# One ring of four PSUM banks, squares of keys from SBUF, and a new order of steps in a cross-attention and quantized feed-forward layer

## The chip, the cores and the metric

The kernel runs on one core of one Trainium2 chip. The metric is the device time of one execution in microseconds, given as the median of several runs. The engines of the core are TensorE (PE: matrix products and transposes, which write only to PSUM; PEld is its loading of weights), VectorE (DVE), ScalarE (ACT), GpSimd (POOL) and SyncE (SP), whose queue issues every transfer of this kernel. PSUM has eight banks; a bank holds one tile of 512 float32 columns on 128 partitions.

## The reference

The layer works on 8 batches of 112 tokens of width 512, with 375 context rows of width 256 for each batch. Attention has 16 heads of 128.

```python
def _L0_xattn_ref(hidden_states, encoder_hidden_states, Wq, Wk, Wv, Wo, gq, gk):
    def rmsnorm(x, g, eps=EPS):
        var = jnp.mean(jnp.square(x), axis=-1, keepdims=True)
        return x * jax.lax.rsqrt(var + eps) * g
    ...
    q = (hidden_states @ Wq).reshape(B, Sq, H, D)
    k = (encoder_hidden_states @ Wk).reshape(B, Skv, H, D)
    v = (encoder_hidden_states @ Wv).reshape(B, Skv, H, D)
    q = rmsnorm(q, gq)
    k = rmsnorm(k, gk)
    scores = jnp.einsum('bqhd,bkhd->bhqk', q, k) * scale
    attn = jax.nn.softmax(scores, axis=-1)
    out = jnp.einsum('bhqk,bkhd->bqhd', attn, v)
    return out.reshape(B, Sq, H * D) @ Wo
...
x = x + _L0_xattn_ref(_layernorm(x, axis=-1), ctx_1024, ...)
x = x + _L0_ffn_ref(_layernorm(x, axis=-1), ...)
```

The feed-forward part rounds its input to 8-bit integers by rows and its weights by one scale, multiplies by W1 (512 to 2048), adds a bias, applies GELU, rounds again by rows, multiplies by W2 (2048 to 512) and adds a bias.

## The kernel before

**Units.** The work is cut into 16 groups G (four pairs of batches times four groups of four heads) and 32 units u (a group and one batch of its pair). A group of four heads is 512 columns wide, which is one bank. A step is a small piece of work on one unit, group or batch, named by letters and a number: `k1.7` makes the second of three tiles of keys of unit 7. Numbers behind the dot are relative to the pair of batches that a script plays; `w0.-1` belongs to the last unit of the pair before.

**The steps of a unit and their engines.** On PE, `k0`, `k1`, `k2` make three tiles of keys (`pkk`, L655). ACT copies each to SBUF (`kc`, into `kk`, L675) and squares it (`kq`, into `ksq`, L681); both read the bank. DVE sums the squares (`kr`, L687); `ka`, `kb`, `ke`, `kd` take the inverse root (ACT and DVE); `kn` scales the keys in `kk` (L694), `kt` transposes their 32 by 32 blocks into `kz` (L704), `ks` sends these to DRAM and `kf` fetches them back as the full transpose `kT`. `kk` has two buffers, so the copies of unit u+2 need the block transposes of unit u to be done. Then come the scores `s0` to `s3` (L764, four banks of their own), their maxima `x` on DVE, exponentials `e` and scaling `n` on ACT, block transposes `z`, and transfers `ps` and `pf`, which give `pT`. `w0`, `w1` weigh the context rows with it (`pu`, L866), and `v0`, `v1` copy the result out (L877). For a group, `Q0`, `Q1` make the queries (`pq`, L537); `S` squares them (L552), `qt` transposes blocks, `qs` and `qf` transfer, `G` applies the gains. `o`, `u` make and copy the values (`po`, L893, L903), `p`, `a` project and add (`pw`, L916, L932); at the very end `O`, `U`, `P`, `A` do the same by halves. `kv`, `qw`, `pt`, `xt`, `ct` and `tp` are transposes on PE, used in the first units, for the last probabilities and in the last feed-forward steps.

**The feed-forward part** of a batch takes the sum of the projections (`ra` or a transfer), adds it to x (`rb`), takes statistics (`st`), an inverse root (`fa` to `fd`), normalizes (`fi`), rounds (`fq`), transposes (`ti`, `tj`, or a transfer), makes the hidden tiles (`h0` to `h3`, L1086; `i`, L1095), applies GELU (`g`), finds the largest (`mx`, `es`), rounds (`qp` on DVE, `qq` on ACT), transposes (`tp`, `tk`), and multiplies by W2 (`Y`, or `y0` and `y1`, L1165; `yo` adds, L1172; `yd` sends).

**What sets the order.** Four scripts, one for each pair, list all steps by hand-written words. `play` (L201) runs them in that order, and `in_written_order` (L77) ties each instruction of PE, DVE, ACT and SP to the one before it on its engine. Nothing overtakes on an engine: an instruction that waits holds up all behind it. Waits between engines follow from tiles: a new tile in a pool waits until the readers of the tile that had its buffer are done.

**PSUM.** Of the eight banks, four hold scores (`ps_sc`), three form a ring `ps_mm` for all products and some transposes, and one, `ps_tr`, holds the warm-up product, transposes at the start (`xt`, `ct`), and some at the end (`ra` of the even batch, `ti`, even `tp`).

Of the kernel before, what the change touches and what calls it, by code (L numbers as in the profile page):

```python
# [30 lines left out]
def xattn_ffn_kernel(  # L31
# [61 lines left out]
    ps_mm = ctx.enter_context(tc.tile_pool(name="ps_mm", bufs=3, space=PSUM))  # L93
    ps_tr = ctx.enter_context(tc.tile_pool(name="ps_tr", bufs=1, space=PSUM))
# [5 lines left out]
    def tr_tile(name):  # L100
        return ps_tr.tile([P, NW], F32, tag="tr", name=name)

    def trh_tile(name, i):
        pool, tag = ((ps_tr, "tr"), (ps_mm, "mm"))[i % 2]
        return pool.tile([P, 2 * NW], BF16, tag=tag, name=name)
# [13 lines left out]
    pw = tr_tile("warm")  # L119
# [279 lines left out]
    def token_turn(b):  # L399
        after(("xm", b))  # L400
        pt = T["pxn", b] = tr_tile(f"pxn_{b}")
        for k in range(KC):
            nc.tensor.transpose(
                pt[:, k * S : (k + 1) * S], tokens_of(b)[:, k * P : (k + 1) * P], ident[:S, :S]
            )
# [67 lines left out]
    def rows_turn(b, j0, j1):  # L473
        pt = T["pc", b] = tr_tile(f"pc_{b}_{j0}")
        for j in range(j0, j1):
            for k in range(KCC):
                nc.tensor.transpose(
                    pt[:, (j - j0) * CC + k * P : (j - j0) * CC + (k + 1) * P],
                    T["cT", b][:, k, j * P : (j + 1) * P], ident,
                )  # L480
# [196 lines left out]
    def key_squares(u, j):  # L677
        if u == 0:
            after(("kh", 1))
        sq = T["ksq", u, j] = work.tile([P, GW], F32, tag="ksq", name=f"ksq_{u}_{j}")  # L680
        nc.scalar.activation(sq, T["pkk", u, j][:, :GW], AF.Square)  # L681
# [280 lines left out]
    def turn_sum(b):  # L962
# [6 lines left out]
        pa = T["pa", b] = (tr_tile, mm_tile)[i](f"pa_{b}")  # L969
# [84 lines left out]
    def turn_rows(what, b, k0, n, i):  # L1054

        pt = T["pt", what, b, k0] = trh_tile(f"p{what}_{b}_{k0}", i)
# [13 lines left out]
    def turn_in(b):  # L1070
        turn_rows("xq", b, 0, KC, 0)
# [73 lines left out]
    def turn_piece(b, n):  # L1145
        after((f"qq{n}", b))
        turn_rows("hq", b, n * (NW // P), NW // P, n)
# [65 lines left out]
    for n in range(2):  # L1213
# [7 lines left out]
        cz.0 lk.0 cz.1 lf.0 lf.1 lx.0 l7.0 lc.1 gl.0 kh.0 lv.0 lk.1 jl.0 lq.0 kh.1 xs.0 xs.1 xa.0 cz.2  # L1221
        xs.7 ct0.0 xa.1 lc.2 xc.1 kc0.0 lq.1 xb.1 xb.7 kq0.0 jl.3 xb.0 kq2.0 k0.1 kr0.0 kc1.0 kr2.0
        kq1.0 xd.1 xc.0 ck0.0 k1.1 xd.0 xa.7 xm.1 kq0.1 xm.0 xc.7 kc2.0 kr1.0 xt.0 xd.7 k2.1 ka.0 ke.0
        kb.0 xk.0 kd.0 kc0.1 kn1.0 kq1.1 xt.1 xm.7 kc1.1 kr0.1 kv1.0 xk.1 kn0.0 kq2.1 xt.7 gm.0 kc2.1
        kn2.0 kv0.0 xk.7 kr1.1 xy.0 k0.2 xl.0 kw0.0 lk.2 kw1.0 lx.1 jm.0 kv2.0 Q0.0 kw2.0 kr2.1 kb.1
        ka.1 ke.1 xy.1 kd.1 kq0.2 kn2.1 kc0.2 kn1.1 k1.2 kn0.1 kt0.1 ct0.1 kc1.2 kt1.1 kq1.2 Q1.0 kt2.1
        ck0.1 qt0.0 ks.1 kr0.2 jm.3 qv0.0 qs0.0 S0.0 jl.1 jl.2 cb0.2 qw0.0 S1.0 k2.2 qv1.0 sb.0 kr1.2
        qx0.0 s3.0 kq2.2 s2.0 sa.0 sc.0 kc2.2 sd.0 ct1.0 s0.0 ck1.0 s1.0 qt1.0 xs.3 qw1.0 qs1.0 kf.1
        kr2.2 k0.3 jl.6 kb.2 ly.0 ka.2 x0.0 ke.2 Q0.1 x1.0 e0.0 kq0.3 kd.2 qx1.0 kr0.3 e2.0 kn2.2 e3.0
        e1.0 k1.3 S0.1 iv.0 kn0.2 kc0.3 kn1.2 n1.0 k2.3 qt0.1 n0.0 cb1.2 qs0.1 n2.0 kt0.2 kq1.3 s2.1  # L1230
        kt2.2 kq2.3 kc1.3 ct1.1 kr2.3 pt0.0 kc2.3 kt1.2 pt1.0 pk0.0 s3.1 n3.0 ks.2 pk1.0 s0.1 kr1.3 s1.1
        x1.1 ka.3 pt3.0 pt2.0 x0.1 lq.2 Q1.1 s7.0 lk.3 pk3.0 e0.1 jm.1 pk2.0 e2.1 e1.1 k0.4 ke.3 e3.1
        kb.3 kd.3 S1.1 kn0.3 kf.2 w0.0 iv.1 qf0.1 kn2.3 n3.1 kq0.4 qt1.1 n0.1 kt0.3 qs1.1 n1.1 kr0.4
        k1.4 xa.3 n2.1 z0.1 sa.1 z2.1 kc0.4 z1.1 kq1.4 k2.4 z3.1 v0.0 sb.1 kc1.4 ps.1 kt2.3 k0.5 kn1.3
        kc2.4 sc.1 kt1.3 kr1.4 ks.3 w1.0 sd.1 jm.2 G0.1 kq2.4 s0.2 lo.0 s1.2 kr2.4 Q0.2 kb.4 ka.4 xs.2
        xc.3 ke.4 v1.0 ja.0 kd.4 kc0.5 pf.1 kn0.4 kq0.5 qf1.1 ck1.1 x0.2 s3.2 e0.2 s2.2 e1.2 kt0.4 kf.3
        k1.5 S0.2 kn2.4 kr0.5 Q1.2 qt0.2 kq1.5 x1.2 qs0.2 js.0 e2.2 kc1.5 e3.2 k2.5 lq.3 kt2.4 S1.2 s7.1
        xb.3 xd.3 iv.2 kn1.4 w0.1 n1.2 lk.4 n0.2 kt1.4 G1.1 z0.2 ks.4 n3.2 js.2 n2.2 jr.0 s3.3 s0.3 cs.2
        qt1.2 s2.3 kq2.5 kr1.5 sa.2 w1.1 kc2.5 z3.2 qs1.2 sc.2 z2.2 v0.1 sb.2 kr2.5 s1.3 z1.2 v1.1 kb.5
        xa.2 x1.3 o0.0 ps.2 sd.2 o1.0 u0.0 js.3 ka.5 ke.5 qf0.2 k0.6 kd.5 xb.2 x0.3 kf.4 Q0.3 kq0.6  # L1240
        kn0.5 lv.1 e0.3 kn1.5 u1.0 js.1 e3.3 kc0.6 e1.3 jr.1 k1.6 e2.3 iv.3 kn2.5 pf.2 p0.0 kq1.6 qt0.3
        S0.3 jr.2 qs0.3 n0.3 xc.2 kt0.5 kc1.6 n3.3 kt2.5 k2.6 G0.2 a0.0 jl.4 n2.3 kr0.6 s0.4 kt1.5 kq2.6
        k0.7 n1.3 z0.3 ks.5 z2.3 kr2.6 s3.4 z1.3 kr1.6 s2.4 qf1.2 z3.3 w0.2 s7.2 ka.6 kc2.6 cz.3 x1.4
        ps.3 kq0.7 ke.6 kb.6 jm.6 s1.4 v0.2 kc0.7 k1.7 kd.6 Q1.3 x0.4 kr0.7 e0.4 xd.2 xm.2 kf.5 kn0.6
# [12 lines left out]
        pf.6 s3.7 u1.2 qs0.4 s2.7 s0.7 x1.7 js.7 lo.2 Q1.4 kf.8 kr2.10 x0.7 kb.10 k0.11 S1.4 kt0.9 sa.4
        ka.10 qt1.4 w0.6 kq0.11 kt1.9 qs1.4 ke.10 sc.4 kt2.9 kd.10 kc0.11 w1.6 kn1.10 v0.6 e0.7 qf0.4
        ks.9 e1.7 e3.7 p1.2 e2.7 iv.7 sb.4 n0.7 lq.5 lk.6 co0.2 z0.7 n1.7 s7.3 n2.7 p0.2 z1.7 co1.2 sd.4
        G0.4 n3.7 v1.6 z3.7 z2.7 kr0.11 s1.8 ps.7 cz.4 s2.8 a0.2 s3.8 jr.5  # L1260
    """, 0)
    play("""
        s0.0 lv.-1 k1.3 a1.-2 qf1.0 kn0.2 kf.1 x1.0 kc1.3 Q0.1 kt0.2 x0.0 kn2.2 k2.3 qt0.1 S0.1 kt2.2
        kq1.3 pf.-1 kt1.2 qs0.1 Q1.1 kq2.3 kr1.3 kr2.3 G1.0 cf.1 e0.0 ka.3 k0.4 e1.0 lq.2 s7.0 xa.2
        kc2.3 ks.2 e2.0 k1.4 e3.0 kq0.4 iv.0 S1.1 s2.1 lo.-1 s3.1 kc0.4 s7.1 sa.1 s1.1 n0.0 qf0.1 s0.1
        ke.3 z0.0 n1.0 qt1.1 co0.1 z1.0 w0.-1 n3.0 kb.3 kd.3 kq1.4 kn1.3 n2.0 sb.1 x0.1 w1.-1 v0.-1
        kc1.4 z2.0 z3.0 kn0.3 ps.0 k2.4 v1.-1 kr0.4 x1.1 o0.-1 kc2.4 kf.2 kt0.3 kq2.4 qs1.1 kn2.3 sc.1
        e0.1 o1.-1 kt1.3 e2.1 xb.3 kr1.4 u0.-1 Q0.2 e1.1 kr2.4 xc.2 kt2.3 e3.1 xb.2 u1.-1 sd.1 ka.4
        jr.-2 xa.3 xc.3 ke.4 G0.1 p1.-1 co1.1 kb.4 kd.4 kn1.4 pf.0 kn2.4 ks.3 jr.-1 iv.1 a1.-1 n2.1 lv.0
        s2.2 S0.2 s1.2 qt0.2 n0.1 s0.2 n1.1 xd.2 qs0.2 p0.-1 z0.1 n3.1 z2.1 z3.1 z1.1 qf1.1 x0.2 ps.1  # L1270
        s3.2 kn0.4 e0.2 k0.5 a0.-1 e1.2 kt0.4 kf.3 w0.0 kc0.5 rz.-2 Q1.2 x1.2 G1.1 kt1.4 e2.2 kq0.5 e3.2
        pf.1 k1.5 v0.0 qf0.2 iv.2 kt2.4 S1.2 rs.-2 n2.2 n3.2 n1.2 s0.3 ks.4 n0.2 s3.3 sa.2 z0.2 kc1.5
        s1.3 z1.2 kq1.5 s2.3 lo.0 w0.1 G0.2 qt1.2 rf.-2 kr0.5 w1.0 x0.3 x1.3 e0.3 kf.4 w1.1 sc.2 lk.3
        v0.1 z2.2 qs1.2 v1.0 xd.3 kr1.5 k2.5 v1.1 z3.2 e2.3 ps.2 o0.0 kq2.5 kr2.5 o1.0 ka.5 e1.3 lc.2
        lq.3 e3.3 kc2.5 iv.3 sb.2 kb.5 n3.3 s3.4 xm.3 n1.3 rn.-2 s1.4 ke.5 xm.2 n0.3 s2.4 zs.-1 u0.0
# [130 lines left out]
```

## Time and profile before

| what | value |
|---|---|
| median of three runs | 730.64 us (730.02 to 731.04) |
| the profiled execution, whole | 731.0 us |
| its span, first to last instruction | 729.0 us |
| mean granted TensorE clock | 0.995 |
| PE busy | 706.7 us, 97% of the span |
| DVE busy | 539.0 us, 74% |
| ACT busy | 431.5 us, 59% |
| mean DMA rate | 258 GB/s |

A row of a group reads: line, engine, operation, output and inputs by name, shapes, count, then busy time, mean ns of one, and the idle time of the engine just ahead with what ended it. A wait row reads: engine, what waited, what it waited for, total us, times, longest us. A row of the chain reads: start, duration, what. A row by stretches reads: the stretch, its length, then busy us and count of PE, PEld, DVE, ACT and POOL, the granted clock, the DMA share and GB/s. Ends of products are modelled, so a product that is held up shows as a longer one; the distance between starts is the safer measure.

### The profile page before, as it was taken

How to read it: one execution, taken by the hardware profiler on the slowest of the kernel's cores; microseconds unless marked ns; L12 is line 12 of the kernel's file. 1: busy time of each engine (PE TensorE's matmuls, PEld its weight loads, DVE VectorE, ACT ScalarE, POOL GpSimd, SP SyncE). 2: the span in 40 equal slices, each digit the busy share in tenths (PEclk: the TensorE clock that was granted, in tenths of full speed). 3: DMA queues.
4: the chain of work that ended last, by engine and by line, in shares of the span. 5: the costliest groups of instructions: out<-in, count | busy, mean ns of one | idle time of the engine just before them, and what ended most of it. 6: DMA issues, size and time to landing. Idle time of an engine off the chain costs nothing.

```text
span 729.0 us, 8599 instructions
## 1 busy us (share of the span) xinstructions
PE 706.7 (97%) x2410; PEld 412.3 (57%) x2410; DVE 539.0 (74%) x1234; ACT 431.5 (59%) x1129; POOL 2.4 (0%) x10
## 2 busy tenths in 40 slices
PE   8999999999999998999999999999999999999976
PEld 4444555745656563746555465564746574567732
DVE  6889898987658486686666578976866799674495
ACT  4677665655476545738455665657656547736225
POOL 0000000000000000000000000000000000000000
PEclk9999999999999999999999999999999999999989
DMA  9889888998898999889798989999999989997100
GB/s 300 271 271 306 271 279 263 316 319 259 284 275 235 309 282 315 270 261 300 190 294 257 297 267 285 277 272 298 246 299 296 255 259 283 222 302 250 30 15 29
DMA packets 131246, 187.85 MB, mean 258 GB/s; under 512 B 34864, under 2 KB 90800, under 8 KB 130560
## 3 DMA queue, kind: packets, MB, share of 16 engines
q1 hardware_dynamic: 131200, 187.32, 84.6%
q8 instruction: 19, 0.31, 0.2%
q14 instruction: 27, 0.22, 0.1%
HBM read 124.55 MB, written 59.45 MB: 252 GB/s over the span
## 4 chain that ended last, share of the span: by engine, by line
PE 83%; DVE 7%; ACT 6%; DMA 3%; issue 1%; SPq 0%; ACTq 0%
PE pu L866 19%; PE pkk L655 17%; PE pw L916 13%; PE pq L537 11%; PE sc L764 10%; PE po L893 6%; PE py L1165 3%; PE ph L1086 2%; DMA pT<-pd 2%; ACT qsq L552 2%; DMA x<-in_x 1%; DVE kss L687 1%; DVE hid L1095 1%; DVE m L1115 1%; ACT kk L675 1%
## 5 line engine op out<-in xcount | busy, mean ns | idle before, releaser
L655 PE MATMUL pkk<-wk,cT 128*128 128x512 f32 x372 | 172.4, 594 | 2.8 <-ACT ksq L681 1.9
L866 PE MATMUL pu<-pT,c 128*128 128x448 f32 (+1 forms) x384 | 152.2, 540 | 2.9 <-ACT kk L675 1.4
L786 ACT ACTIVATE probs<-sc,bias,rq 112x375 f32<-112x375 f32 x128 | 84.6, 668 | 56.8 <-DVE bias L779 56.2
L866 PEld LDWEIGHTS pu<-pT,c 128*128 128x128 f32 (+1 forms) x384 | 72.4, 190 | 73.2 <-issue 61.8
L655 PEld LDWEIGHTS pkk<-wk,cT 128*128 128x128 f32 x372 | 69.7, 189 | 77.6 <-issue 63.7
L916 PEld LDWEIGHTS pw<-oT,wo 128*128 128x128 f32 x544 | 98.1, 190 | 9.1 <-issue 6.7
L537 PE MATMUL pq<-wq,xnT 128*128 128x512 f32 x224 | 100.9, 593 | 2.4 <-ACT ksq L681 1.7
L916 PE MATMUL pw<-oT,wo 128*128 128x224 f32 (+1 forms) x544 | 102.0, 343 | 0.2 <-ACT oT L903 0.2
L764 PE MATMUL sc<-kT,qT 128*112 128x384 f32 x256 | 92.1, 488 | 0.7 <-ACT qT L584 0.6
L687 DVE TENSOR_REDUCE kss<-ksq 128x4 f32<-128x512 f32 x96 | 63.6, 670 | 32.1 <-ACT ksq L681 32.0
L803 DVE STREAM_TRANSPOSE pz<-probs 128x384 f32<-128x384 f32 x120 | 63.4, 555 | 23.5 <-ACT probs L797 21.4
L797 ACT ACTIVATE probs<-probs,inv 112x375 f32<-112x375 f32 x128 | 72.4, 605 | 12.4 <-DVE inv L794 12.3
L777 DVE TENSOR_REDUCE top<-sc 112x1 f32<-112x375 f32 x128 | 63.5, 535 | 20.8 <-PE sc L764 20.7
L675 ACT COPY kk<-pkk 128x512 f32<-128x512 f32 x96 | 55.8, 584 | 34.7 <-PE pkk L655 27.9
L537 PEld LDWEIGHTS pq<-wq,xnT 128*128 128x128 f32 x224 | 42.1, 190 | 51.8 <-issue 45.4
L681 ACT ACTIVATE ksq<-pkk 128x512 f32<-128x512 f32 x96 | 56.8, 597 | 24.3 <-PE pkk L655 21.1
L764 PEld LDWEIGHTS sc<-kT,qT 128*112 128x112 f32 x256 | 44.5, 177 | 40.4 <-issue 12.6
L877 ACT COPY wc<-pu 128x448 f32<-128x448 f32 x64 | 33.3, 531 | 56.8 <-PE pu L866 56.8
L694 DVE TENSOR_TENSOR kk<-kk,rk 128x512 f32<-128x512 f32 x96 | 62.7, 676 | 0.7
L704 DVE STREAM_TRANSPOSE kz<-kk 128x512 f32<-128x512 f32 x93 | 62.0, 688 | 0.6
L893 PEld LDWEIGHTS po<-wc,wv 128*128 128x128 f32 x272 | 48.9, 190 | 9.1 <-issue 4.8
L893 PE MATMUL po<-wc,wv 128*128 128x224 f32 (+1 forms) x272 | 52.9, 344 | 0.7 <-ACT ksq L681 0.6
(122 smaller groups left out, 595.6 us busy)
## 6 DMA issues: line engine op xcount, KB each, us to landing
kd<-kz SPq DMA_DIRECT2D x124, 192.0 KB, 3.7
kT<-kd SPq DMA_DIRECT2D x31, 768.0 KB, 6.3
pT<-pd SPq DMA_DIRECT2D x30, 672.0 KB, 6.1
pd<-pz SPq DMA_DIRECT2D x90, 192.0 KB, 3.4
wq<-in_wq SPq DMA_DIRECT2D x16, 1024.0 KB, 7.0
wo<-in_wo SPq DMA_DIRECT2D x16, 1024.0 KB, 7.4
wv<-in_wv SPq DMA_DIRECT2D x16, 512.0 KB, 6.3
wk<-in_wk SPq DMA_DIRECT2D x15, 512.0 KB, 6.5
```

Of the source, the lines that this page charges most:

```text
L537: nc.tensor.matmul(pq[:, :GW], T["xnT", p][:, k, i * P : (i + 1) * P], T["wq", G][:, k, :], start=(k == 0), stop=(k == KC - 1),)
L655: nc.tensor.matmul(pk[:, :GW], T["cT", batch_of(u)][:, k, j * P : (j + 1) * P], T["wk", u // BP][:, k, :], start=(k == 0), stop=(k == KCC ...
L675: nc.scalar.copy(T["kk", u][:, j, :], T["pkk", u, j][:, :GW])
L687: nc.vector.tensor_reduce(T["kss", u][:, j, :], T.pop(("ksq", u, j)).rearrange("p (h d) -> p h d", d=D), AX.X, ALU.add)
L764: nc.tensor.matmul(sc[:S, :SKP].rearrange("p (j i r) -> p j i r", j=NJ, r=BK), T["qT", G, i][:, h, :], T["kT", u][:, :, :, h, :].rearrange ...
L777: nc.vector.tensor_reduce(top[:, h : h + 1], T["sc", u, h0 + h][:S, :SK], AX.X, ALU.max, negate=True)
L786: nc.scalar.activation(p_bufs[h][:S, :SK], T["sc", u, h][:S, :SK], AF.Exp, bias=T["bias", u, h0][:, h - h0 : h - h0 + 1], scale=rq_of(u, h ...
L797: nc.scalar.mul(p_bufs[h][:S, :SK], p_bufs[h][:S, :SK], T["inv", u][:, h : h + 1])
L803: nc.vector.transpose(T["pz", u][:, :, :, :, h, :].rearrange("p a f j q -> p j a f q"), p_bufs[h].rearrange("p (j a r) -> p j a r", j=NJ, ...
L866: nc.tensor.matmul(pu[:, : HG * S], T["c", b][: ROWS[j], j, k * P : (k + 1) * P], T["pT", u][: ROWS[j], :, j, :, :].rearrange("p f h q -> ...
L893: nc.tensor.matmul(po[:, (h - h0) * n : (h - h0 + 1) * n], T["wv", G][:, k, h * D : (h + 1) * D], T["wc", G][:, k, h, :, :].rearrange("p b ...
L916: nc.tensor.matmul(pw[:, (c - c0) * n : (c - c0 + 1) * n], T["wo", G][:, h, c * P : (c + 1) * P], T["oT", G][:, h, lo : lo + n], start=(h ...
```

## The change

All products and transposes share one ring of four banks; `ps_tr` is gone. The squares of keys read the copy in SBUF, so they follow the copy, and the bank is free once the copy is done. The four scripts hold the same steps in a new order. The core of the diff, with the end of the last script (the other scripts are new in the same way):

```diff
-    ps_mm = ctx.enter_context(tc.tile_pool(name="ps_mm", bufs=3, space=PSUM))
-    ps_tr = ctx.enter_context(tc.tile_pool(name="ps_tr", bufs=1, space=PSUM))
+    ps_mm = ctx.enter_context(tc.tile_pool(name="ps_mm", bufs=4, space=PSUM))
     ps_sc = ctx.enter_context(tc.tile_pool(name="ps_sc", bufs=4, space=PSUM))
 
     def mm_tile(name):
         return ps_mm.tile([P, NW], F32, tag="mm", name=name)
 
-    def tr_tile(name):
-        return ps_tr.tile([P, NW], F32, tag="tr", name=name)
-
-    def trh_tile(name, i):
-        pool, tag = ((ps_tr, "tr"), (ps_mm, "mm"))[i % 2]
-        return pool.tile([P, 2 * NW], BF16, tag=tag, name=name)
+    def mmh_tile(name):
+        return ps_mm.tile([P, 2 * NW], BF16, tag="mm", name=name)
...
-        pt = T["pxn", b] = tr_tile(f"pxn_{b}")
+        pt = T["pxn", b] = mm_tile(f"pxn_{b}")
...
-        pt = T["pc", b] = tr_tile(f"pc_{b}_{j0}")
+        pt = T["pc", b] = mm_tile(f"pc_{b}_{j0}")
...
     def key_squares(u, j):
-        if u == 0:
-            after(("kh", 1))
+        after((f"kc{j}", u))
         sq = T["ksq", u, j] = work.tile([P, GW], F32, tag="ksq", name=f"ksq_{u}_{j}")
-        nc.scalar.activation(sq, T["pkk", u, j][:, :GW], AF.Square)
+        nc.scalar.activation(sq, T["kk", u][:, j, :], AF.Square)
...
-        pa = T["pa", b] = (tr_tile, mm_tile)[i](f"pa_{b}")
+        pa = T["pa", b] = mm_tile(f"pa_{b}")
...
-        pt = T["pt", what, b, k0] = trh_tile(f"p{what}_{b}_{k0}", i)
+        pt = T["pt", what, b, k0] = mmh_tile(f"p{what}_{b}_{k0}")
...
-        a1.2 w0.6 w1.6 pk2.7 lm.-1 v0.6 pt1.7 v1.6 pt3.7 pk1.7 O0.3 pk3.7 qh0.-1 w0.7 U0.3 qh1.-1 te.-1
-        w1.7 P0.3 v1.7 v0.7 O1.3 A0.3 ra.0 U1.3 P1.3 rb.0 st.0 fb.0 fa.0 fc.0 fd.0 fi.0 y0.-1 fq.0 bo.0
-        ti.0 y1.-1 A1.3 tj.0 ra.1 yo.-1 h0.0 rb.1 yd.-1 st.1 h1.0 i0.0 fa.1 h2.0 fc.1 i1.0 g0.0 h3.0
...
+        v0.6 qh0.-1 pt2.7 v1.6 pt1.7 qh1.-1 pk2.7 O0.3 pk1.7 te.-1 w0.7 U0.3 P0.3 v0.7 w1.7 A0.3 ra.0
+        v1.7 O1.3 rb.0 st.0 fb.0 U1.3 fa.0 P1.3 fc.0 fd.0 fi.0 fq.0 A1.3 ti.0 bo.0 ra.1 tj.0 rb.1 h0.0
+        st.1 h1.0 i0.0 fa.1 fc.1 h2.0 i1.0 g0.0 fb.1 h3.0 i2.0 fd.1 g2.0 fi.1 fq.1 i3.0 ti.1 y0.-1 tj.1
...
+        Y0.0 mx2.1 tk1.0 tp2.0 g3.1 mx1.1 Y1.0 tk2.0 mx3.1 tk3.0 Y2.0 es.1 qp2.1 Y3.0 qp0.1 qq2.1 qp3.1
+        qq0.1 qp1.1 qq3.1 tp0.1 yo.0 qq1.1 tp3.1 tp2.1 yd.0 tk0.1 tp1.1 tk2.1 Y0.1 tk1.1 bo.1 Y1.1 tk3.1
+        Y2.1 Y3.1 yo.1 yd.1
```

The first script of the new order begins with:

```
cz.0 lk.0 cz.1 lf.0 lf.1 lx.0 l7.0 gl.0 lc.1 kh.0 jl.0 lk.1 lq.0 jl.3 jl.6 kh.1 xs.1 xs.0 xa.1
xc.1 xs.7 ct0.0 kc0.0 xa.0 xb.7 k0.1 kc1.0 xb.1 xd.1 xc.0 xm.1 xa.7 kq0.0 xc.7 k1.1 kr0.0 kq1.0
...
```

and that of the old order with:

```
cz.0 lk.0 cz.1 lf.0 lf.1 lx.0 l7.0 lc.1 gl.0 kh.0 lv.0 lk.1 jl.0 lq.0 kh.1 xs.0 xs.1 xa.0 cz.2
xs.7 ct0.0 xa.1 lc.2 xc.1 kc0.0 lq.1 xb.1 xb.7 kq0.0 jl.3 xb.0 kq2.0 k0.1 kr0.0 kc1.0 kr2.0
...
```

Here `lk`, `lq`, `lv`, `lc`, `lf`, `lx` load weights, context and tokens, `jl` loads a piece of the feed-forward weights (1024 KB), `jm` takes its maximum on DVE (L320), `js` and `jr` scale and round it, and `xs` to `xm` normalize the tokens (`xa` and `xc` are the root's two ACT instructions).

## The prediction

> **What bounds the kernel now.** I read the page's busy times first, then the chain that ended last, then the waits of PE by stretch, then the chain at single stalls.
>
> ```profile
> PE 706.7 (97%) x2410; PEld 412.3 (57%) x2410; DVE 539.0 (74%) x1234; ACT 431.5 (59%) x1129; POOL 2.4 (0%) x10
> PE 83%; DVE 7%; ACT 6%; DMA 3%; issue 1%; SPq 0%; ACTq 0%
> ```
>
> PE is the bound, so a new order can only win what PE loses. The busy time hides part of that loss, since a product that starts late is drawn longer. The chain shows what a step costs when nothing holds it: 4 instructions of keys 1.72 us, 8 of queries 3.43, 6 of `pu` 2.26, 8 of scores 2.58, 16 of `po` or `pw` 3.03, 16 of the feed-forward 3.45; the halves of the last group take 1.8 (16 `po`) and 3.55 (32 `pw`). With the counts of the groups (384, 224, 384, 256, 240, 480, 224, then 32 and 64) that is 165.1 + 96.0 + 144.6 + 82.6 + 45.5 + 90.9 + 48.3 + 10.7, and some 10 for all transposes: 693.7 us. The span is 729.0, so 35.3 us are not product time: 4.7 before the first keys, 4.4 after the last product, and 26.2 between. Start times in the timeline put 4.6 of these before 50 us, 9.9 between 50 and 650, and 11.7 after. The waits of PE between 50 and 660 us (total, times, longest):
>
> ```profile
> PE pq L537 <- ACT ksq L681: 1.7, 1, 1.7
> PE pu L866 <- ACT kk L675: 1.4, 1, 1.4
> PE pu L866 <- DMA pT<-pd: 0.9, 2, 0.6
> PE pq L537 <- ACT qsq L552: 0.7, 1, 0.7
> PE pu L866 <- ACT wc L877: 0.6, 1, 0.6
> PE po L893 <- ACT ksq L681: 0.6, 1, 0.6
> PE pkk L655 <- ACT ksq L681: 0.4, 1, 0.4
> PE pkk L655 <- ACT oT L903: 0.4, 1, 0.4
> ```
>
> These are 6.7 us. Seven of the eight rows, 5.8 us, name an ACT instruction that reads *another* tile than the one the product needs: keys hold up queries, keys hold up `pu`. That is a bank not yet free. Two such places in the chain (start, us, what):
>
> ```profile
> 279.09 0.59 ACT kk L675
> 279.68 0.51 ACT probs L797
> 280.19 0.49 ACT ksq L681
> 280.73 3.70 PE pq L537 x8
> ```
>
> ```profile
> 81.76 1.89 ACT wff L341
> 83.65 0.48 ACT ksq L681
> 84.13 0.19 ACT rs_t L361
> 84.32 0.48 ACT kk L675
> 84.84 2.52 PE pu L866 x6
> ```
>
> In the first the copy of the keys is done at 279.68, but the bank is held until the squares, behind a softmax step, end a microsecond later. In the second a 1.9 us rounding sits ahead of both readers. The product after a wait takes 2.52 instead of 2.26 us: each wait costs 0.26 more than its row. So the seven rows are worth 5.8 + 7 x 0.26 = 7.6 us, the DMA row 0.9 + 2 x 0.26 = 1.4: together 9.0 of the 9.9.
>
> The end is another regime: from 700 us PE works half the time and DVE nearly all of it.
>
> ```profile
> 700.00:710.00 10.00, 5.29 (x20) 1.99 (x19) 9.51 (x27) 4.08 (x7) 0.00 (x0) 0.71 0.05 16
> ```
>
> **The change, part by part.** Both scripts hold the same 2482 steps, so no work goes and none comes; every queue (PE, DVE, ACT, SP) has its old instructions in a new order. POOL keeps its two weight maxima in their order.
>
> *The fourth bank.* I counted, for every tile taken from the ring of product banks, how much PE work (by the durations above) stands between the last product into the bank's old tile and the first into the new: the time that the readers have. Before, over 302 turns of three banks, the median is 4.7 us; after, over 315 turns of four, 7.3. In the trace a key tile is freed a median 3.1 us after its last product ends, nine in ten within 5.5 us. Between 50 and 650 us of product time, 151 of 250 turns have under 5.5 us before, 38 of 249 after. Scaling the ring's 7.6 us by 38/151 leaves 1.9: a gain of 5.7. The transposes that now share the ring stand in the first 50 us and at the end alone, and are in these counts.
>
> *Squares from SBUF.* 60 of the 96 squares stood before their copy, so there the copy freed the bank and its move changes nothing; where the squares came last the bank is now free earlier. The copy alone ends a median 2.6 us after the products, against 3.1 for both. The price on ACT:
>
> ```profile
> L681 ACT ACTIVATE ksq<-pkk 128x512 f32<-128x512 f32 x96 | 56.8, 597 | 24.3 <-PE pkk L655 21.1 <-DVE kss L687 2.0 <-ACT probs L786 0.8
> L675 ACT COPY kk<-pkk 128x512 f32<-128x512 f32 x96 | 55.8, 584 | 34.7 <-PE pkk L655 27.9 <-DVE kz L704 6.4
> ...
> L442 ACT COPY xnT<-xr 128x512 f32<-128x512 f32 x5 | 3.1, 613 | 2.5 <-DMA xr<-xd 2.5
> ```
>
> The nearest row for a source in SBUF is the 613 ns copy, 29 ns over the one from PSUM: 96 x 29 ns = 2.8 us. The bounds are 0 (squares keep 597) and 8.6 us (90 ns each, the overlap of two independent ACT instructions that a square right behind its own copy loses; 10 stand so). I take 2.8. ACT is idle 297 us, which covers it; if the cover were gone, it would cost PE at most those 8.6.
>
> The Trainium skill, "ScalarE: Activation LUTs", section "Step-by-step: what each stage is for", speaks against this part: it says that ScalarE sits closer to PSUM and VectorE closer to SBUF. The 613 against 584 ns agrees in sign. The page's own price for a 512-wide instruction with immediate operands (186 ns + 0.833 ns per element, section "What ACT_TABLE_LOAD costs") is an estimated 613 ns wherever the source lies; by it the squares would cost ACT 1.5 us in all, with the same end time, as both figures stay under the idle time.
>
> *The new order, middle.* The lead from the last product of a unit's keys to its first scores grows from a median 36 to 53 us of PE work. That buys cover for the key chain, but the copies of keys write one of two buffers, freed by the block transposes on DVE of two units earlier. In the script the first copy follows the last of these with no PE work between in 12 of 29 units, before in 3. ACT then waits for DVE, and behind that copy stand softmax and other evacuations. Before, this wait is 6.4 us of ACT time in three times. I take 0.7 us of the gain back for it, two thirds of one stall with its restart: 5.0 net (bounds: 7.6 at best; the loss of the last rival below). The DMA stalls stay: a fetch of probabilities lands in 6.1 us, and the script leaves its user a median 6.5 us in both orders, the shortest 3.4 before and 3.0 after. Weight loads are within 1 us of their old leads (shortest 5.4 to 5.6 for keys, 7.3 to 7.0 for queries). Scores behind the query fetch win: the shortest lead from fetch to gain goes from 1.3 to 4.5 us.
>
> *The head.* Before, PE loses 1.5 us at 12.1 us, because the first copy of keys waits on ACT behind a root that needs x; after, another root and its exponential still stand ahead of it, but only the copy frees the bank: about 1 us won. The stall of 0.6 us for the first scores goes, as 1.7 us of keys now stand ahead of them. Against it, the first 2.27 us maximum of the weights now stands on DVE ahead of the last key norm of unit 0, whose transpose PE awaits: about 0.9 us lost, and 0.4 for two bank turns of the transposes that lose their own bank. On SP a 1024 KB weight piece moves ahead of the keys' second weights, and the values' 512 KB go behind; their users come 8 us and more later. Sum +0.3, bounds -1.5 and +1.5.
>
> *The tail.* Let T be the start of the first half-group of values (677.8 in the trace). The order before: values, 12 `pu`, 32 `pw`, values, transpose of the sum (T+12.3 us done). After: values, 6 `pu`, 32 `pw`, 6 `pu`, transpose: 1.8 + 2.26 + 3.55 + 2.26 + 0.43 = T+10.3. The next 32 `pw` end at T+16.8 instead of T+16.1, as the second values now wait some 0.8 us with nothing beside them. The DVE chain of the first batch takes 5.58 us in the trace (690.17 to 695.75), so it ends at T+15.9; then the add (0.61) at T+17.6, bias 0.68, copy 0.42, and the second residual starts at T+18.7 instead of T+20.85: 2.1 won. The output add (0.75) and 16 `py` that stood ahead of it go into later gaps, so 0.6 comes back: the last scale stands at T+39.0 instead of T+40.5. After it the script puts all four roundings (4 x 0.66) ahead of the first copy on ACT; the first output product starts 3.7 us after the scale instead of 2.4, and the four then run unbroken: 7.3 us to their end, instead of 6.6. Net 1.5 - 0.7 = 0.8 won (bounds -0.7 and +2.5).
>
> The sum against the profiled execution (729.0 span plus 2.0 around it = 731.0; the median of the three runs is 730.64, 0.4 lower): 731.0 - 5.0 - 0.3 - 0.8 = 724.9, rounded to 725.0.
>
> **The rivals.**
> - *Ring stalls vanish altogether.* All 7.6 us, 1.5 in the head, 1.5 in the tail: 720.4. For it: only 3 middle turns are left under 3.1 us, the median release, before 16. Against it: ACT bursts of 1.9 us and table loads still stand in the queue.
> - *The waits only move to the transfers.* PE, running ahead, meets the pT fetch (6.1 us against a lead of 6.5 at the median), and DMA engines are 0.82 to 0.98 busy in the middle. The longest such wait now is 0.6 us; one of 0.5 with its restart at eight of 30 fetches gives back 6.1 us, all of the gain: 731. Against it: PE's wait for DMA is 0.9 us now.
> - *Slower: ACT held behind DVE.* The copies of keys wait for the block transposes in the 12 tight units. If each wait reaches PE as a 0.8 us stall plus restart, 12 x 1.06 = 12.7 us against 5.7 + 0.3 + 0.8 = 6.8 won: 736.9. It decides from 7 such stalls on. For it: 12 tight units in place of 3, on a DVE that is 74% busy. Against it: DVE's work by the rows passes a 20 us stretch in five stretches of the new order and six of the old, and the ring's leads are 2.6 us longer.
>
> **How the numbers follow.** My forecast 0.62 (its own range 721 to 728.5), ring stalls gone 0.14, moved to transfers 0.10, slower 0.14. A measurement here tells about 0.2%, 1.5 us, from no change: 729.2 to 732.1 is "same". Faster 0.76, same 0.10, slower 0.14. The range runs from 718.5, just past the second case, to 732.0, which leaves out most of the slower case and little else.
>
> **What would show it.** Right: PE's waits for `ksq` gone from the middle, waits of PE between 50 and 660 us near 2 us, mostly DMA; the ring's last readers still ACT copies; `ksq` near 613 ns; the second batch's residual starting 2 us earlier against the first values. Wrong: PE waiting in sum as long for `kk` or `wc` as now, ACT's waits for `kz` well over 6.4 us, or a gap after the roundings at the end over 1 us longer than worked out.

## The result, and the profile after

The changed kernel takes 720.97 us (median of 6 runs, 720.28 to 725.34); the kernel before, on the same chip, 730.31 us (729.82 to 731.04). The ratio is 0.987 (95% interval 0.9855 to 0.9888), so 9.3 us are won. The forecast was 725.0 us. The profiled execution took 720.28 us, with a span of 718.5.

The busy times and the chain of the page:

```profile
PE 702.7 (98%) x2398; PEld 413.3 (58%) x2410; DVE 537.3 (75%) x1234; ACT 433.6 (60%) x1129; POOL 2.4 (0%) x10
...
PE 85%; DVE 5%; ACT 4%; DMA 3%; SPq 1%; issue 1%; POOL 0%; ACTq 0%; DVEq 0%; POOLq 0%
```

The span shrank by 10.5 us, the busy time of PE by 4.0 only (12 of its 2410 products are missing from this trace, so count little on that figure); a product that isn't held up is drawn shorter. The shares of DVE and ACT in the chain fell from 7 and 6% to 5 and 4%.

The waits of PE between 50 and 660 us (total us, times, longest), where the kernel before had eight rows and 6.7 us:

```profile
PE pu L860 <- DMA pT<-pd: 1.0, 1, 1.0
PE pkk L650 <- DVE hid L1089: 0.3, 1, 0.3
PE sc L758 <- DMA kT<-kd: 0.2, 1, 0.2
```

No row names the reader of a bank of the keys or queries any more; 1.2 of the 1.5 us are transfers, and the 0.3 us that are left are the ring still: keys wait for the reader of a hidden tile's bank. Behind 660 us:

```profile
PE pxq L1052 <- DVE xq L1039: 3.2, 1, 3.2
PE phq L1052 <- ACT hq L1137: 1.6, 3, 0.8
PE py L1159 <- ACT hqT L1060: 0.9, 1, 0.9
PE pw L910 <- ACT oT L897: 0.6, 1, 0.6
```

The first row is PE waiting for the last batch's rounded input, 4.2 us before. Two groups of ACT, and a wait of ACT:

```profile
L670 ACT COPY kk<-pkk 128x512 f32<-128x512 f32 x96 | 55.2, 580 | 58.6 <-DVE kz L698 25.6 <-PE pkk L650 25.4 <-PE sc L758 5.7
...
L675 ACT ACTIVATE ksq<-kk 128x512 f32<-128x512 f32 x96 | 59.5, 628 | 6.4 <-DVE kss L681 6.0
```

```profile
ACT kk L670 <- DVE kz L698: 25.6, 12, 6.4
```

A square costs 628 ns from SBUF (597 from PSUM), and ACT stands 25.6 us, in 12 places, before the copies of keys until the block transposes on DVE have freed `kk` (before: 6.4 us in 3 places).

**A measure for what follows.** As in the prediction, I count what PE loses by the distance between the starts of its products, less their undisturbed durations (693.7 us for all). Three stretches: the head (the products of the first 50 us), the middle (those up to 640 us of product time), the end. The end I also give as the time from the first half values (`O0`) to the end of the span, which needs no such count.

| profile | head | middle | from `O0` to the end |
|---|---|---|---|
| before | 4.62 | 9.86 | 51.3 |
| changed | 2.87 | 2.87 | 49.4 |

So in this pair of profiles the head won 1.75 (0.34 of which a later start of the first keys took back), the middle 7.0, the end 1.9 to 2.2 depending on the measure. The forecast had 0.3, 5.0 and 0.8. The experiments show how much of each is the change, and how much is the execution that happened to be profiled.

### The profile page after: what moved, and what is told of

It is laid out like the page before. It is cut to its first block, busy times and chain, and to the rows that moved or that the text cites. A ratio compares the mean times of both kernels' runs of the same rounds, so it can differ in the third digit from the quotient of the medians.

```text
span 718.5 us, 8555 instructions
## 1 busy us (share of the span) xinstructions
PE 702.7 (98%) x2398; PEld 413.3 (58%) x2410; DVE 537.3 (75%) x1234; ACT 433.6 (60%) x1129; POOL 2.4 (0%) x10
## 4 chain that ended last, share of the span: by engine, by line
PE 85%; DVE 5%; ACT 4%; DMA 3%; SPq 1%; issue 1%; POOL 0%; ACTq 0%; DVEq 0%; POOLq 0%
PE pkk L650 19%; PE pu L860 17%; PE pw L910 13%; PE pq L532 12%; PE sc L758 10%; PE po L887 6%; PE py L1159 2%; PE ph L1080 2%; DMA pT<-pd 1%; PE pkk L660 1%; DMA kT<-kd 1%; ACT probs L780 1%; DMA qr<-q 1%; DMA qss<-s 1%; ACT qsq L547 1%
## 5 line engine op out<-in xcount | busy, mean ns | idle before, releaser
L860 PE MATMUL pu<-pT,c 128*128 128x448 f32 (+1 forms) x384 | 152.3, 540 | 1.0 <-DMA pT<-pd 1.0
L860 PEld LDWEIGHTS pu<-pT,c 128*128 128x128 f32 (+1 forms) x384 | 72.5, 190 | 71.3 <-issue 61.7
L670 ACT COPY kk<-pkk 128x512 f32<-128x512 f32 x96 | 55.2, 580 | 58.6 <-DVE kz L698 25.6
L675 ACT ACTIVATE ksq<-kk 128x512 f32<-128x512 f32 x96 | 59.5, 628 | 6.4 <-DVE kss L681 6.0
```

Source lines behind the costliest of these rows:

```text
L860: nc.tensor.matmul(pu[:, : HG * S], T["c", b][: ROWS[j], j, k * P : (k + 1) * P], T["pT", u][: ROWS[j], :, j, :, :].rearrange("p f h q -> ...
```

## The experiments

My theory was that the fourth bank wins the middle, because the product behind an evacuation no longer waits for it, and that the squares and the order add little there. The main rivals: the squares carry the gain (the bank comes free earlier), or the order does. Parts of the change can't be applied at will, since the order fixes which bank is free when: the new order with three banks for products would let a product wait for a reader that stands behind it. So the parts were built on the old order, and the end was exchanged by itself.

In these kernels a script word `!4` lets all products and transposes share four banks from there on, and `!3` ends it:

```diff
+    def bank(own):
+        if ring["banks"] == 3:
+            return own
+        ring["turn"] += 1
+        return (ps_tr, "tr") if ring["turn"] % 4 == 0 else (ps_mm, "mm")
```

### The fourth bank alone, the squares alone, and both

The bank (`!4` behind the transposes of the first contexts, `!3` ahead of the end):

```diff
-        pf.1 kn0.4 kq0.5 qf1.1 ck1.1 x0.2 s3.2
+        pf.1 kn0.4 kq0.5 qf1.1 ck1.1 !4 x0.2 s3.2
...
-        v1.6 pt3.7 pk1.7 O0.3 pk3.7 qh0.-1
+        v1.6 pt3.7 pk1.7 !3 O0.3 pk3.7 qh0.-1
```

> The kernel before, its order and its squares untouched, but from the first unit's last transposes to the first half-group of values the products rotate over four banks: the bank of the transposes, idle in between, joins the three. Theory (the fourth bank is what won in the middle, whatever the order): turns of the ring with under 5.5 us of product time fall from 151 to 54 of 250, so the 7.6 us of ring stalls between 50 and 650 us fall to about 2.7 and the time by 4 to 6.5 us, to about 724 to 726; PE's waits for ksq, kk, wc and oT between 50 and 660 us, now 5.8 us, fall under 2. Rival (the new order won, since it spreads the readers; a bank alone moves each wait to the next turn, ACT being as late as before): under 2 us won, 728.5 to 730.5, and PE waits still name ACT for 4 us or more.

Measured: 724.68 us, 0.990 of the time before (0.9880 to 0.9913). Its waits of PE between 50 and 660 us:

```profile
PE pu L886 <- DMA pT<-pd: 1.9, 2, 1.4
PE sc L784 <- ACT ksq L701: 0.7, 1, 0.7
PE sc L784 <- DMA kT<-kd: 0.2, 1, 0.2
```

The waits of queries and context products for readers of a bank are gone with the bank alone; what is left is two fetches of probabilities, and waits of the scores, which have banks of their own. The row of 0.7 us is a fetch too, by its times: the fetch of `kT` for these scores is issued at 528.2 us and lands after 6.7, and they start at 535.06.

The squares (the 36 of 96 that already stood behind their copy read it):

```diff
-        nc.scalar.activation(sq, T["pkk", u, j][:, :GW], AF.Square)
+        nc.scalar.activation(sq, T["kk", u][:, j, :] if copied else T["pkk", u, j][:, :GW], AF.Square)
```

> The kernel before, its order and its three banks untouched, but the 36 of the 96 squares that stand behind their own copy read the copy in SBUF, so that these banks are free once copied. Theory (a bank held by late squares is part of the ring's stalls): the three stalls of PE for ksq in the middle, 1.7, 0.6 and 0.4 us with 0.26 each of restart, go or shrink to the copy's end, 1 to 3 us won, 727.5 to 729.5, and the squares of these 36 take near 630 ns instead of 597. Rival (the copy is the one that frees most banks, and ACT loses the overlap): within 1 us of 730.3, or slower.

Measured: 728.58 us, 0.995 (0.9937 to 0.9965). The rows of the middle, the largest three:

```profile
PE pu L889 <- ACT kk L688: 1.9, 2, 1.4
PE sc L787 <- DMA kT<-kd: 0.8, 1, 0.8
PE pq L550 <- ACT kk L688: 0.7, 1, 0.7
```

No product of the middle waits for a square now, but the 1.7 us row of queries for `ksq` has become 0.7 us for `kk`: the copy is the next reader.

> Both of these in the order of before: four banks in the middle and 36 squares from SBUF. Theory: little more than four banks alone, 723.5 to 726, since with four banks few turns still end on late squares. If the two parts add up fully, 722 to 724. If the order is what counts, 728 to 730.

Measured: 724.40 us, 0.989 (0.9879 to 0.9908), the same as the bank alone. So the bank wins some 1.0% by itself and the squares 0.5% by themselves, and together 1.06%: with four banks there is nothing left for the squares to win. The table gives PE's loss for all three.

| profile | head | middle | from `O0` to the end |
|---|---|---|---|
| bank | 4.83 | 4.10 | 50.7 |
| squares | 4.74 | 7.06 | 51.7 |
| both | 4.99 | 3.09 | 51.4 |

### The new order with squares from PSUM again

```diff
-        after((f"kc{j}", u))
+        copied = (u, j) in FROM_COPY
+        if copied:
+            after((f"kc{j}", u))
...
-        nc.scalar.activation(sq, T["kk", u][:, j, :], AF.Square)
+        nc.scalar.activation(sq, T["kk", u][:, j, :] if copied else T["pkk", u, j][:, :GW], AF.Square)
```

`FROM_COPY` lists the other 55.

> The changed kernel in its new order, but 41 of the 96 squares of keys read the bank in PSUM again (those whose place in the order lets them); the other 55 read the copy. Banks are held longer by these 41. Theory (with four banks the ring has leads enough, so who frees a bank last doesn't matter): within 0.1% of the changed kernel, 0.986 to 0.988 of the time before, and no wait of PE for a square of keys over 1 us in all. Rival (the squares from SBUF carry the gain, as 0.49% for 36 of them on three banks suggests): about 0.991, with waits of PE for squares of 2 us and more.

> The changed kernel, unaltered, as the base of its three neighbours and for a tighter ratio. Expected: 0.987 of the time before, as in its first comparison (0.9872, 0.9855 to 0.9888).

Measured on the same chip: 720.48 us with 41 squares from PSUM, 0.985 (0.9829 to 0.9871), against 721.86 us for the changed kernel, 0.987 (0.9846 to 0.9887). Reading PSUM is at least as good. Of its waits in the middle one names a square, 0.4 us. The rival (0.991) fell; the time lies just under the 0.986 to 0.988 of the theory, within the scatter. With four banks it makes no difference that shows which reader frees them last, and the source of the squares is no part of the gain that these runs show.

### The end by itself

The first attempt put the new end behind the old order, with `!4` ahead of `O0.3`. For that, steps on both sides of the seam, where the old order meets the new end, had to change places:

```diff
-        pt1.7 v1.6 pt3.7 pk1.7 O0.3 pk3.7 qh0.-1 w0.7 U0.3 qh1.-1 te.-1 w1.7 P0.3
+        pt1.7 v1.6 pt3.7 pk3.7 qh0.-1 qh1.-1 !4 O0.3 pk1.7 te.-1 w0.7 U0.3 P0.3 v0.7 w1.7
...
```

> The kernel before, with only the end of its last script, from the first half-group of values on, in the new order and on four shared banks. By the working of the prediction 0.8 us are won (1.5 up to the last scale, 0.7 given back by the roundings put ahead of the first copy): 729.5. By the traces of both kernels, which lose 11.7 and 9.5 us of product time after 640 us, 2.2 us are won: 728. Rival (the tail wins nothing by itself, and the new kernel's end is only better because more was ready at its start): 730 to 731.

Measured: 733.38 us, 1.002 (1.0005 to 1.0026), slower. Its chain at the seam (start, us, what):

```profile
678.38 0.51 DVE pT L860
...
679.18 1.30 DVE hid L1150
...
680.50 1.23 DVE hq L1153
681.73 0.43 DVE pT L860
...
682.29 4.15 PE pu L886 x6
```

The copy of the last probabilities (`pk1.7`, L860) now stands on DVE behind 2.5 us of roundings of an earlier batch, and PE, with nothing else in its queue, stands still until 682.29. The wait is mine, not the change's: in the changed kernel these roundings come well before. So this run doesn't price the new end. Two cleaner ones followed: the changed kernel with the old end, and the old order with the bank and the new end, but with the seam as the old order has it.

The changed kernel with the old end:

```diff
-        n1.7 pk3.7 v0.6 qh0.-1 pt2.7 v1.6 pt1.7 qh1.-1 pk2.7 O0.3 pk1.7 te.-1 w0.7 U0.3 P0.3
+        n1.7 v0.6 pt2.7 v1.6 pt1.7 pk2.7 pk1.7 !3 O0.3 pk3.7 qh0.-1 w0.7 U0.3 qh1.-1 te.-1 w1.7 P0.3
...
```

The old order with the bank and the new end:

```diff
-        pt3.7 pk1.7 O0.3 pk3.7 qh0.-1 w0.7 U0.3 qh1.-1 te.-1 w1.7 P0.3 v1.7 v0.7
+        pt3.7 pk1.7 O0.3 pk3.7 qh0.-1 w0.7 U0.3 qh1.-1 te.-1 P0.3 v0.7 w1.7
...
```

> The changed kernel with its end undone: from the first half values (O0.3) on, the steps stand in the old order, on three product banks and one for transposes; all before that is the new order on four banks, squares from SBUF. Theory (the new tail wins 2.1 us by itself, as the start times of the two traces say): 0.9872 + 2.1/730 = 0.990 of the time before. By the prediction's own size of the tail (0.8 us): 0.988. Rival (the tail gained because the middle delivered its work earlier, not by its order): 0.987, as the changed kernel.

> The old order with the fourth bank shared by products from the first context transposes on to the end, squares of keys from PSUM where they stood, and the new order of steps for the end alone, behind the first half values; the last copies of probabilities and the roundings of the feed-forward batch before stay where the old order has them. Theory (bank 7.5 us, tail 2.1 us, and the two don't share a stall): 0.9896 - 2.1/732 = 0.9867 of the time before, so 722.4 on a chip where before takes 732.1; what is then left to the changed kernel is its head. Rival (the new tail wins nothing in the old order, as the first attempt at it, 1.0016, says): 0.990.

Measured: with the old end 723.24 us, 0.988 (0.9860 to 0.9902), so 1.4 us (by the medians) over the changed kernel on that chip, of which some 0.4 are a wait of PE at the new seam, for a copy of the last probabilities; bank and new end 723.52 us, 0.989 (0.9868 to 0.9908), against 0.990 for the bank alone. Neither distance is outside its intervals, but both have the sign and size of the prediction's 0.8 us rather than of the 2 us that the first pair of profiles showed.

| profile | head | middle | from `O0` to the end |
|---|---|---|---|
| changed, second time | 2.46 | 4.30 | 50.2 |
| 41 squares from PSUM | 2.02 | 3.16 | 50.1 |
| changed, old end | 2.75 | 4.47 | 50.6 |
| old order, bank, new end | 4.71 | 3.10 | 49.9 |

### The clock at the end

The second profile of the changed kernel has an end that is 0.8 us longer than the first (50.2 against 49.4 us). The windows around PE's 3.2 us wait show why (us, then busy us and count of PE, PEld, DVE, ACT, POOL, the granted clock, DMA share, GB/s). The first profile:

```profile
692.00:694.00 2.00, 0.00 (x0) 0.00 (x0) 1.86 (x6) 0.29 (x1) 0.00 (x0) 1.00 0.00 0
694.00:696.00 2.00, 1.35 (x10) 0.76 (x11) 1.97 (x5) 0.71 (x2) 0.00 (x0) 1.00 0.00 0
696.00:698.00 2.00, 2.00 (x11) 0.94 (x10) 1.97 (x5) 0.44 (x1) 0.00 (x0) 1.00 0.04 8
```

The second:

```profile
694.00:696.00 2.00, 0.33 (x5) 0.34 (x6) 1.86 (x7) 0.00 (x0) 0.00 (x0) 0.95 0.00 0
696.00:698.00 2.00, 2.00 (x7) 0.71 (x6) 2.00 (x5) 1.15 (x2) 0.00 (x0) 0.50 0.04 8
698.00:700.00 2.00, 2.00 (x8) 0.79 (x7) 1.60 (x6) 0.00 (x0) 0.00 (x0) 0.69 0.00 0
```

And the kernel before, around its 4.2 us:

```profile
704.00:706.00 2.00, 0.00 (x0) 0.00 (x0) 1.86 (x6) 0.62 (x2) 0.00 (x0) 0.55 0.00 0
706.00:708.00 2.00, 1.32 (x6) 0.63 (x7) 1.89 (x5) 0.00 (x0) 0.00 (x0) 0.50 0.00 0
708.00:710.00 2.00, 2.00 (x6) 0.76 (x5) 1.90 (x7) 0.00 (x0) 0.00 (x0) 0.50 0.00 0
710.00:712.00 2.00, 2.00 (x12) 0.86 (x10) 2.00 (x6) 1.33 (x2) 0.00 (x0) 0.74 0.00 0
```

PE stands still, the granted clock falls to 0.50, and the products behind the wait, the last batch's hidden tiles, run at half speed: 7 products in 2 us instead of 11. In two kernels I filled the wait with products that nobody reads:

```diff
     def turn_in(b):
+        if b == B - 1:
+            idle = ps_sc.tile([P, NW], F32, tag="sc", name="idle")
+            for n in range(10):   # 14 in the kernel before
+                nc.tensor.matmul(idle, ident_h, w1q[:, 0, :NW], start=True, stop=True)
         turn_rows("xq", b, 0, KC)
```

> The kernel before, nothing changed but 14 products that nobody reads (some 3.0 us) in the 4.2 us in which PE waits for the last batch's rounded input; there the clock was 0.50 from 704.4 to 711 us, and three hidden tiles each cost 0.8 to 0.9 us more than at full clock. Theory: the clock stays 1.00 and up to 2.5 us are won, of which VectorE's own work on these tiles hides a part: 0.997 to 0.9985 of the time before. Rival (the slowed products are hidden behind VectorE altogether): 1.000.

Measured: 730.45 us, 0.998 (0.9968 to 0.9991) of the time before: 1.7 us won by 14 products without use. The window that stood at 0.50 before, in this kernel:

```profile
708.00:710.00 2.00, 1.47 (x10) 0.67 (x9) 2.00 (x5) 0.00 (x0) 0.00 (x0) 1.00 0.00 0
```

From `O0` to the last product it takes 46.1 us, before 47.1. So the fallen clock cost the kernel before some 1.0 us at its end by this pair of profiles, and the theory holds there.

> The changed kernel with 10 products that nobody reads (128x512, some 2.15 us by the feed-forward's own row) in the 3.2 us in which PE waits for the last batch's rounded input at the end. In the first profile of the changed kernel the granted clock stayed 1.00 behind this wait, in the second it was 0.50 for 3.3 us and the end took 0.8 us longer. Theory (the clock falls because PE is idle some 3 us, and the last batch's hidden tiles then pay): granted clock 1.00 in every microsecond behind the wait, 50.16 - 0.8 = 49.4 us from the first half values to the end, and 0.9866 - 0.8/730 = 0.9855 of the time before, with less scatter. Rival (the clock falls for another reason, or the tiles it slows are hidden behind VectorE): the clock still falls, or it doesn't and the time stays at 0.9866.

Measured: 722.38 us, 0.987 (0.9851 to 0.9886). The clock is 1.00 in every microsecond behind the wait and the end takes 49.4 us, as the theory had it, but the time is that of the changed kernel, which the rival named, and the scatter is no smaller (721.22 to 724.16). In the profile PE lost 7.2 us in the middle, where the changed kernel, with the same instructions up to there, lost 2.9 and 4.3. That explains this one execution, the slowest of the four, and not their median; the interval holds both 0.9855 and 0.9866. So no gain of the idle products is shown in the changed kernel, and none is ruled out.

### What is left in the middle

Five profiles have the new order unaltered up to 640 us. At the scores `s2` of unit 25, one place among several, they show this:

| profile | fetch of `kT` issued at | wait of PE there | middle in all |
|---|---|---|---|
| changed | 529.9 | 0.2 | 2.87 |
| changed, second time | 530.9 | 0.8 | 4.30 |
| changed, old end | 531.8 | 1.6 | 4.47 |
| changed, filled | 533.6 | 1.8 | 7.22 |
| changed, another end (below) | 533.5 | 1.8 | 6.24 |

The chain of the second profile up to that place (start, us, what; the lines are steps of SP's queue, L600 the queries' send, L807 that of probabilities):

```profile
527.56 0.41 SPq L600
...
528.96 0.54 SPq L807
...
529.54 1.32 SPq L807
...
530.90 6.43 DMA kT<-kd
...
537.47 0.87 PE sc L758 x2
```

The fetch takes 5.8 to 6.4 us in all five profiles; it is late where it stands longer on SP behind the sends of queries and probabilities. In the filled kernel, where it is latest, SP's timeline reads:

```profile
521.82 5.34 SPq L1077 DMA_TRANSPOSE hqT<-hq  x1
527.25 1.97 SPq L587 DMA_DIRECT2D qd<-qz  x4
...
530.82 2.78 SPq L807 DMA_DIRECT2D pd<-pz  x4
533.65 0.47 SPq L714 DMA_DIRECT2D kT<-kd  x1
```

Here the issue of a transposing transfer holds SP's queue for 5.3 us ahead of all of them. (In that profile the wait is charged to a copy on ACT, 1.8 us; the fetch, issued at 533.6, lands after 5.8 us, at 539.4, and the scores start at 539.6. I read the wait as the fetch.) That issue isn't what sets the executions apart: in the first profile, where the scores wait 0.2 us, it takes 5.46 us, but starts at 517.99. Why SP is later in one execution than in another was not tried.

### An end that was meant to be better, and all together

Two of the last batch's four roundings go from ACT to DVE, and the output products follow half by half:

```diff
+        if b == B - 1 and n % 2:
+            nc.vector.tensor_scalar(T["hq", b][:, cols], T["hid", b][:, cols], MAGIC, Q, ALU.subtract, ALU.min)
+        else:
             nc.scalar.activation(T["hq", b][:, cols], T["hid", b][:, cols], AF.Identity, bias=neg_magic)
...
-        es.1 qp2.1 Y3.0 qp0.1 qq2.1 qp3.1 qq0.1 qp1.1 qq3.1 tp0.1 yo.0 qq1.1 tp3.1 tp2.1 yd.0 tk0.1
-        tp1.1 tk2.1 Y0.1 tk1.1 bo.1 Y1.1 tk3.1 Y2.1 Y3.1 yo.1 yd.1
+        es.1 qp0.1 Y3.0 qq0.1 qp1.1 qq1.1 tp0.1 tk0.1 tp1.1 qp2.1 tk1.1 qq2.1 Y0.1 qp3.1 qq3.1 tp2.1
+        tk2.1 Y1.1 tp3.1 tk3.1 yo.0 yd.0 bo.1 Y2.1 Y3.1 yo.1 yd.1
```

> The changed kernel with another end: of the last batch's four roundings, two go from ACT to DVE, each followed at once by its transposes, which use the score banks; the output products of the last batch follow half by half. Worked out from the rows, the 7.15 us from the last scale to the last output product shrink by 1.1 to 1.35 us: theory 0.9866 - 1.2/730 = 0.985 of the time before. Rival (the two roundings on DVE meet the copies of the transposes there, and the end stays as long): 0.9866.

Measured: 722.43 us, 0.987 (0.9851 to 0.9892): nothing won. The last products end 6.4 us after the start of the scale (710.30 to 716.74), in the filled kernel 7.2 (710.99 to 718.23), so 0.8 us of the hoped-for 1.1 to 1.35 are there. But DVE's last additions read:

```profile
715.40 0.74 DVE L1170 SCALAR_TENSOR_TENSOR y<-py,d,x 128x512 f32<-128x512 f32 x1
...
718.73 0.75 DVE L1170 SCALAR_TENSOR_TENSOR y<-py,d,x 128x512 f32<-128x512 f32 x1 [1.99 <-DMA out<-y]
```

The last addition waits 2.0 us for a transfer: `y` has one buffer, I had moved the even batch's addition and send (`yo.0`, `yd.0`) behind the odd batch's transposes, and the last addition can't write before that send is through. The products ended earlier, and the output later: 50.5 us from `O0` to the end instead of 49.4.

> All that looked good in one kernel: the new order with 41 of the squares from PSUM (0.985), the idle products at the end (-0.8 us when the clock would fall), the other end (-1.2 us), and the first maximum of the weights moved on DVE behind the last key norm of unit 0, for which PE waits 0.4 to 0.5 us in every profile of the new order (-0.6 us with its restart). Theory (the four add): 0.985 - 2.6/730 = 0.9815. Rival (each of them only moves the wait): 0.985.

Measured: 722.76 us, 0.987 (0.9856 to 0.9891). The four don't add. Its end has the same wait for `y`, and with the clock at 1.00 it takes 50.5 us. In its head PE's wait for the last key norm (0.4 us) is gone, but 1.1 us are lost at 12.0 us, at the first bank of the keys, as in the kernel before; whether the moved maximum did that or the arrival of the first transfers can't be told from one profile. No kernel that I ran is shown to beat the changed one: the nearest, with 41 squares from PSUM, has an interval that overlaps it.

## Why the prediction was right, and where not

The forecast (725.0, range 718.5 to 732.0, faster 0.76) held in sign and range, and was 4 us too slow. By its own steps:

**The fourth bank (5.7 us won).** Right in cause: the bank alone gives 0.990. The size came from the turns with short leads, which left 1.9 us of the ring's waits. That step was too cautious: of the ring's rows one is left, 0.2 to 0.3 us in each profile, so it came near to the first rival. But PE meets the transfers instead: DMA rows of PE's waits in the middle come to 1.2, 3.0, 2.9, 2.9 and 2.3 us in the five profiles of the new order, 0.9 in the profile before. In the last two of the five, rows of the scores that are charged to ACT end as a fetch of keys lands (at 539.4 us, and at 499.0 and 602.6); with them it is 4.7 and 4.5 us. So the second rival, waits that move to the transfers, is there in part, with keys' fetches rather than the probabilities' that it named. The prediction looked at the lead of the probabilities' fetch alone and missed that of `kT`. The two errors partly cancel. Three profiles with the old middle lose 9.86, 10.52 and 11.13 us there (the last two are the first attempt at the end and the filled kernel before), a mean of 10.5; the five of the new order lose 5.0. That is 5.5 us won, where 5.0 were forecast, and the 7.0 of the first pair was a lucky execution. (The last two of the five are of executions 1.8 and 2.2 us above their kernels' medians, the old ones up to 1.2, so 5.5 is itself good to about 1 us.)

**Squares from SBUF.** 31 ns more than from PSUM were measured, 29 were taken, and no run shows that it costs PE anything. The prediction left open what their earlier release would win; it is nothing with four banks, and 0.5% with three. The Trainium skill's 186 ns + 0.833 ns per element ("ScalarE: Activation LUTs", section "What ACT_TABLE_LOAD costs"), an estimated 613 ns for either source, lies between the 597 and 628 ns that the two kernels show; it can't tell the sources apart.

**The new order in the middle (0.7 us lost to copies behind `kz`).** The coupling came as counted, 12 places, and larger than feared on ACT, 25.6 us. ACT's waits for `kz` well over 6.4 us were named as a sign of being wrong; they came, and the gain came all the same. None of it reached PE in the waits between 50 and 660 us shown above: four banks cover it. The step failed in its charge to PE, and the slower rival, which rested on the same count, fell with it. That the order wins nothing else in the middle was not foreseen: the old order with the bank loses 4.1, 3.1 and 3.1 us there, the new one 5.0 in the mean.

**The head (0.3 us won).** This is the step that was most mis-sized. Seven profiles with the old head lose 4.4 to 5.0 us there (mean 4.7), five with the new one 2.5 to 3.0 (mean 2.75): 2.0 us, more than the bound of 1.5. Of the terms, the stall at the first bank is 1.7 us by starts and goes in four of the five, 0.4 being left in the filled kernel (1.0 was taken), the one before the first scores is 0.8 (0.6), and one of 0.6 at 45 us, an ACT copy, was not in the sum and goes too. The new wait for the last key norm costs 0.6 (0.9), the two bank turns 0.1 (0.4). One loss was not foreseen: a transpose of probabilities that starts 0.8 us late at 47 us. Another, 0.6 to 1.0 us in the first keys of four of the five profiles, isn't the order's: these products start 0.85 us apart instead of 0.43 until the trace's first clock record, which stands at 6.3 to 7.2 us there and at 4.2 in the fifth. The profiles of the old order have the same, 0.0 to 1.05 us, but there it shortens the stall at the first bank (1.7 us in the profile before, 0.6 to 0.9 where the keys lose 0.5 us or more, with 1.2 in one). The prediction's trace was thus of an execution in which that stall is long. No run exchanged the head alone; the nearest, the bank and the new end behind the old head and middle, is 1.7 us slower than the changed kernel on the same chip, with intervals that overlap.

**The end (0.8 us won).** The second residual stands 18.5 us behind `O0` (forecast 18.7), the gap behind the last scale is 7.2 us (7.3). (The prediction's own terms for the end of the second half's projections add up to T+16.5 rather than its T+16.8; they end at T+17.0.) The last scale, forecast at T+39.0, stands at 38.0 in the first profile of the changed kernel and at 38.8 in the second. The clean runs give about 1 us for the order: with the clock at 1.00 on both sides, the filled kernels need 46.1 us in the old order and 45.2 in the new one from `O0` to the last product, so 0.9. What the prediction didn't see is the clock: the profile it was made from has the clock down for 6.8 us at the end, the first profile of the changed kernel not at all. That made 0.9 into 1.9 in this pair of profiles.

Together: 5.5 in the middle, 2.0 in the head, and 1.2 at the end (the mean of four new ends, 49.9 us, against five old ones, 51.1, clock included) are 8.7 of the 9.3 us. The rest is within the scatter of the executions.

## What to carry to other kernels

Before weighing an order of steps, count the buffers that it turns over: one more bank left nothing in the middle for two other repairs of the same waits (earlier release, more distance in the order) to win, and the earlier release, tried alone on three banks, won 0.5% and would have looked like the cause. When PE stops waiting for buffers it meets the next thing behind it, here the queue that issues the transfers; so check the lead of every fetch, not of the one that shows a wait today. And one profile on each side is not enough to price a stretch of 50 us: the same instructions lost 2.9 to 7.2 us in five executions, which no single pair could have told from the change.

## What the runs showed of the hardware

**An idle PE gets half a clock, and in the kernel before it paid to keep it busy with nothing.** Behind the 4.2 us wait of the old end the granted clock fell to 0.50 in five profiles of five, for 3.4 or 6.8 us; behind the 3.2 us wait of the new end in three of six; behind 1.1 to 1.2 us, filled, in none of three. Products for nobody won 1.7 us (0.9968 to 0.9991) in the kernel before. The Trainium skill ("TensorE: Matmul & The Clock Gate", section "Part 1: The HAM clock gate (the "warmup" mystery)") tells of a free-running window of 3.4 us, whose end may fall anywhere in a kernel. The traces agree: in all 14 profiles every stretch at one clock that lies whole inside the profile lasts a multiple of 3.413 us, and the grid lies elsewhere in each. Laid on that grid, the waits sort themselves. In all eight of these falls the 3.4 us just ahead of the fall held only 0.1 to 0.9 us of products. In the three new ends without a fall, an end of the grid split the 3.2 us wait, 1.4 us or more of products were left on both sides, and the clock stayed at 1.00. One row doesn't fit: in the first attempt at the end, PE stood still from 680.43 to 682.29 us, 1.9 us, and the clock was 0.50 until 685.6, although the 3.4 us ahead of that fall held some 1.5 us of (narrow) products. Why is open.

**The issue of a transposing transfer holds the queue.** One `hqT<-hq` kept SP for 5.34 us (in the first profile of the changed kernel its five issues take 1.3 to 5.5 us), while the fetches behind it took 0.4 to 0.7 us each to issue.

**The source of an ACT instruction shows.** 128x512 squares took 597 ns from PSUM and 628 from SBUF, in profiles of 96 each; side by side in the kernel with 36 of them from SBUF, 592 and 629.
